# Text order instead of the scheduler's on PE, ACT and DVE, and a third buffer for the batches' rows

## The chip, the core and the metric

The kernel runs on one core of a Trainium2 chip. The metric is the device time of one execution in microseconds (us). Besides the plain times there is a profile: one execution recorded by the hardware profiler, with the start and duration of every instruction on every engine. The engines are PE (TensorE, matrix products and transposes; PEld is its loading of weights), DVE (VectorE), ACT (ScalarE), POOL (GpSimd) and SP (SyncE, which here only issues DMAs).

## What is computed

Eight batches of 2048 rows with 128 channels pass through four graph-attention layers that share one 2048 x 2048 adjacency. Each layer is preceded by a layer norm and a ReLU, and its result is added to x.

```
h = relu(layernorm(x));  x = x + layer0(h)    # GAT, then elu
h = relu(layernorm(x));  x = x + layer1(h)    # GAT
h = relu(layernorm(x));  x = x + layer2(h)    # 4 heads, scores = h_head @ h_head.T
h = relu(layernorm(x));  x = x + layer3(h)    # node weights, W, layernorm, GAT, residual, elu

GAT:    Wh = h @ W;  e[i, j] = leaky_relu(Wh[i] @ a1 + Wh[j] @ a2)
        out = softmax(where(adj > 0, e, -big)) @ Wh
heads:  e = leaky_relu(h_head @ h_head.T);  out = softmax(where(adj == 0, -inf, e)) @ h_head
```

All of it is in float32. In the second kind of layer there are four heads of 32 channels.

## The kernel before, in words

**Units and streams.** One batch in one layer is a *unit*; there are 32. Layers 0, 1 and 3 are units of class `Gat` with 16 steps, layer 2 is a unit of class `Heads` with 64 steps (four groups of 512 query rows by 16 blocks of keys). The even batches form stream a and the odd ones stream b, and the units of the two alternate: a layer 0, a layer 1, b layer 0, a layer 2, b layer 1, a layer 3, b layer 2, then layer 0 of a's next batch, b layer 3, a layer 1, b layer 0, a layer 2 and so on. So a `Heads` unit follows either a layer 0 or a layer 3 of the other stream, four times each, and a layer 3 is prepared during a layer 1 (four times) or a layer 0 (three times). The last layer 3 has nothing beside it.

**Steps.** A step has a `front` and a `back`. In `Gat`, the front makes two blocks of unnormalised attention weights on DVE (L459, twice: maximum with a spread row, times the edge mask), and the back multiplies them on PE into PSUM (L472: 16 products in the text, 32 instructions in the trace, as a float32 product takes two). In `Heads` the front makes scores on PE (L543), exponentials on ACT (L546) and the masked weights on DVE (L548); the back multiplies them with the values on PE (L557). Three `z` buffers hold the weights between front and back. In the text a front is written two steps ahead of its back (`AHEAD = 2`).

**Pieces.** While a unit runs, the next one is prepared: `begin` returns a list of pieces, and the loop calls them in proportion to the steps done (`room` is four steps fewer than the unit has). The pieces are: `first` (load x), `stats` four times (L195 and L196 per block of 128 rows), `end` (`moments_end`: L201 on DVE, the power on POOL L203, L205 on DVE), `rows` (L247, ACT), for layer 3 `scaled` (L254, DVE), for layer 2 `kept` (L258), `turned` (transposes L267 on PE, copy L270 on ACT, for layer 2 the low part L272 on DVE), for layer 2 `stacked` (16 DMAs on SP's queue, L281 and L282, that build `hi_lo` and `lo_hi`), else `project` (L291 on PE, then L396 to L398 on ACT and L303 on DVE, or for layer 3 L298 and L299), for layer 3 a second set of statistics and `normed` (L325) and `weighted` (L330), at last `spread` (L342 on PE, L343 on ACT).

**Ends of a unit.** When half of a `Gat` unit is summed, `out_first` takes the reciprocals (L409) and scales the sums out of PSUM (L413 on DVE, or L416, L417, L419 on ACT). The rest waits in a list for some steps (`later`): `out_elu` (L445, L446) for layer 0, `out_norm` (L426 to L428 on DVE, L430, L431 on ACT) and then `out_elu` and the store (L436, SP's queue) for layer 3. At the end of a group `Heads` copies its sums to `o_t` (L562, ACT), and `out` transposes them (L569), normalises (L572, L574) and adds them to x (L576).

**What sets the order.** In the kernel before, the scheduler of the tile framework orders the instructions of each engine: the text's order is a priority for it, and it may draw an instruction ahead of others. Each engine then runs its list in that order and waits at semaphores.

**Buffers.** `big` has two buffers a name unless told otherwise; x has two, `o` two, `z` three. PSUM is one tile of eight banks: scores use pairs 6, 4 and 2 in turn, sums banks 5, 6, 7 and 2, 1, 0, pieces beside a `Gat` unit banks 3 and 4 alone.

The loop that makes the text's order:

```
for s in range(u.steps):
    if s + AHEAD < u.steps:
        u.front(s + AHEAD)
    elif overlaps and not (u.layer != 2 and nxt.layer == 2):
        nxt.front(s + AHEAD - u.steps)
    elif overlaps and s == u.steps - 1:
        turn[0] = 2
        nxt.front(0)
    u.back(s, later)
    while done < total and done < total * (s + 1) / room:
        pieces[done]()
        done += 1
    pass_time(u.us)
```

Of the kernel before, what the change touches and what calls it, by code (L numbers as in the profile page):

```python
# [8 lines left out]
F32 = mybir.dt.float32  # L9
# [5 lines left out]
OP = mybir.AluOpType  # L15
PSUM = bass.MemoryType.PSUM

P = 128
HEADS = 4
HD = 32  # L20
# [15 lines left out]
def adj_preln_d4(ctx: ExitStack, tc: tile.TileContext, x, adj, w0, a0, w1, a1, w3, a3,  # L36
# [12 lines left out]
    nc = tc.nc  # L49
    B, N, C = x.shape  # L50
    NB = N // P
    HB = NB // 2
# [4 lines left out]
    const = ctx.enter_context(tc.tile_pool(name="const", bufs=1))  # L57
# [15 lines left out]
    def load(src, shape, name):  # L73
        t = const.tile(shape, F32, name=name)
        nc.scalar.dma_start(out=t, in_=src)
        return t
# [12 lines left out]
    beta_sb = load(beta.partition_broadcast(P), [P, C], "beta_sb")  # L89
# [24 lines left out]
    nc.vector.tensor_copy(tot3, pw[:, :4])  # L114
    nw1_sb = const.tile([P, NB], F32, name="nw1_sb")
    nc.vector.tensor_scalar(nw1_sb, nw_sb, 1.0, None, op0=OP.add)
    beta2_sb = const.tile([P, C], F32, name="beta2_sb")
    nc.vector.tensor_scalar(beta2_sb, beta_sb, 2.0, None, op0=OP.mult)

# [17 lines left out]
    def run(ctx, general):  # L139
        stat = ctx.enter_context(tc.tile_pool(name="stat", bufs=2))  # L140
        big = ctx.enter_context(tc.tile_pool(name="big", bufs=2))
# [10 lines left out]
        def score_banks():  # L152
            turn[0] = (turn[0] + 1) % 3
            return SCORES[turn[0]]
# [4 lines left out]
        def half_tile(name):  # L159
            return big.tile([P, HB, C], F32, tag=name, name=name)  # L160


        X = {}

        def load_x(b):
            X[b] = big.tile([P, NB, C], F32, tag="x", name="x")
            nc.sync.dma_start(out=X[b], in_=x[b].rearrange("(n p) c -> p n c", p=P))

        load_x(0)


# [36 lines left out]
        class Unit:  # L208
# [5 lines left out]
            def begin(self, banks):  # L214
# [4 lines left out]
                def first():  # L219
                    if b not in X:  # L220
                        load_x(b)
                    self.xb = X[b]
                    self.st = stat.tile([P, NB, 6], F32, tag="st", name="stx")
                    self.mv = stat.tile([P, NB, 2], F32, tag="mv", name="mvx")
# [200 lines left out]
            def out_norm(self, half, xs, a, later):  # L425
                nc.vector.tensor_add(a, a, self.wh[:, half * HB:(half + 1) * HB, :])  # L426
                nc.vector.tensor_mul(a, a, gamma_sb[:, None, :].to_broadcast([P, HB, C]))
                nc.vector.tensor_add(a, a, beta2_sb[:, None, :].to_broadcast([P, HB, C]))  # L428
                e = half_tile("oe")
                nc.scalar.activation(e, a, AF.Exp)  # L430
                nc.scalar.activation(a, a, AF.Relu)  # L431

                def last():
                    self.out_elu(xs, a, e)
                    lo = half * HB * P
                    nc.sync.dma_start(  # L436
                        out=out[self.b, lo:lo + HB * P, :].rearrange("(n p) c -> p n c", p=P),
                        in_=xs)
                    if half == 1:
                        del X[self.b]  # L440
                later(6.0, last)
# [87 lines left out]
        class Heads(Unit):  # L529
# [35 lines left out]
            def out(self, g, pair, o_t):  # L565
                lo = score_banks()
                pv = ps[:, lo, :].rearrange("p (k e) -> p k e", k=4)
                for k in range(4):
                    nc.tensor.transpose(pv[:, k, :], o_t[:, k * P:(k + 1) * P], ident)  # L569
                pv = pv.rearrange("p k (h e) -> p k h e", h=2)  # L570
                r = stat.tile([P, 4, 2, 1], F32, tag="r2", name="r2")
                nc.vector.reciprocal(r, pv[:, :, :, HD:HE])  # L572
                o = big.tile([P, 4, 2, HD], F32, tag="o", name="o")
                nc.vector.tensor_mul(o, pv[:, :, :, :HD], r.to_broadcast([P, 4, 2, HD]))  # L574
                xs = X[self.b][:, g * 4:g * 4 + 4, pair * 64:(pair + 1) * 64]
                nc.vector.tensor_add(xs, xs, o.rearrange("p k h d -> p k (h d)"))  # L576
# [10 lines left out]
        def later(us, f):  # L587
            waiting.append([us, f])
# [50 lines left out]
    ok = nc.values_load(near_i[0:1, 0:1], min_val=0, max_val=1)  # L639
    with tc.If(ok > 0) as arm:  # L640
        with ExitStack() as inner:
            run(inner, False)
    with arm.Else():
        with ExitStack() as inner:
# [25 lines left out]
```

## Time and profile before

| what | value |
|---|---|
| median of 2 runs | 3565.78 us (3564.5 to 3567.05) |
| the profiled execution | 3565.65 us, its span 3563.8 us |
| mean granted clock of PE | 0.959 |
| DMA over the span | 70.96 MB, 20 GB/s |
| largest group: L472 on PE | 1415.6 us busy, 12288 instructions |
| L557 and L543 on PE | 1014.6 and 503.6 + 440.9 us busy |
| L548 and L459 on DVE | 1171.7 and 949.0 us busy |
| L546 on ACT | 1086.3 us busy |

The span runs from the first to the last recorded instruction; the device time is 1.85 us longer. Busy time counts what an engine executes, not what it waits. In a row of the groups, "out<-in" are the program's names of the tiles, then come the count, the busy time with the mean duration of one, and the idle time of the engine just before them with what ended it. In a timeline each row has its start, its duration, the engine, line and operation, and in brackets the idle time before it and what released it. Operations of one engine can overlap in the record: the next one starts before the last has left the pipeline.

### The profile page before, as it was taken

Reading aid. Unit: us, or ns where it says so; the run is one execution under the profiler, and the core shown is the slowest. Engines: PE = TensorE matmul, PEld = TensorE weight load, DVE = VectorE, ACT = ScalarE, POOL = GpSimd, SP = SyncE. Lnnn points to the kernel's source line nnn. Section 1 sums busy time; section 2 is a strip of 40 time slices with the busy share of each in tenths; the row PEclk is TensorE's granted clock in tenths of the full one; section 3 lists DMA queues with packets and bytes.
Section 4 is the critical chain, followed back from the end, with each engine's and each line's share of the span. In section 5 each row is a group of like instructions: output and inputs, shape, how many; then the busy total and the mean of one; then the engine's idle time right before and its main releaser. Section 6 shows DMA issues by size and latency. Waiting matters only on the chain.

```text
span 3563.8 us, 53234 instructions
## 1 busy us (share of the span) xinstructions
PE 3312.8 (93%) x22669; PEld 2222.9 (62%) x22669; DVE 2673.9 (75%) x3586; ACT 1681.7 (47%) x2521; POOL 135.1 (4%) x47
## 2 busy tenths in 40 slices
PE   4798999999999899989999899999999989999997
PEld 3787337734899435943599834783379953495337
DVE  3666778777888677877787677877788767787776
ACT  4113663376422565356542276427652246624661
POOL 0000000000000000000000000000000000010000
PEclk7888999999999899999999999999999989999998
DMA  6002000300000200030000200020000020002000
GB/s 216 1 1 48 1 1 1 72 1 1 1 25 1 48 1 1 1 72 1 1 1 25 48 1 1 1 68 5 1 1 7 19 48 1 1 1 60 1 1 14
DMA packets 35511, 70.96 MB, mean 20 GB/s; under 512 B 8000, under 2 KB 25024, under 8 KB 29120
## 3 DMA queue, kind: packets, MB, share of 16 engines
q1 hardware_dynamic: 29312, 67.12, 7.3%
q8 instruction: 179, 2.93, 0.3%
q10 hardware_dynamic: 5952, 0.35, 0.1%
q14 instruction: 68, 0.56, 0.1%
HBM read 25.51 MB, written 8.39 MB: 10 GB/s over the span
## 4 chain that ended last, share of the span: by engine, by line
PE 77%; DVE 11%; ACT 5%; POOL 2%; DMA 2%; issue 2%; POOLq 0%; ACTq 0%; DVEq 0%; SPq 0%
PE ps L472 30%; PE ps L557 25%; PE ps L543 16%; DVE z L459 5%; PE ps L291 3%; POOL rstdx L203 2%; ACT z L546 2%; PE ps L267 2%; PE ps L342 1%; DVE z L548 1%; ACT hw L247 1%; DVE stx L195 1%; ACT wh L325 1%; DMA raw<-in_adj_dram 1%; PE ps L569 1%
## 5 line engine op out<-in xcount | busy, mean ns | idle before, releaser
L548 DVE TENSOR_TENSOR z<-z,edge_t 128x2048 f32<-128x2048 f32 x512 | 1171.7, 2292 | 433.6 <-ACT z L546 433.6
L472 PE MATMUL ps<-y,z 128*128 128x129 f32 x12288 | 1415.6, 276 | 4.3 <-DVE z L459 4.3
L472 PEld LDWEIGHTS ps<-y,z 128*128 128x128 f32 x12288 | 1399.9, 193 | 8.4 <-DVE z L459 4.5
L546 ACT ACTIVATE z<-ps,shift 128x1024 f32<-128x1024 f32 x1024 | 1086.3, 1111 | 428.9 <-PE ps L543 408.4
L557 PE MATMUL ps<-z,hv 128*33 128x512 f32 x4096 | 1014.6, 605 | 5.1 <-DVE z L548 4.4
L459 DVE SCALAR_TENSOR_TENSOR z<-r,cr,edge_t 128x1024 f32<-128x1024 f32 x768 | 949.0, 1275 | 92.2 <-PE ps L472 80.6
L543 PE MATMUL ps<-hi_lo 64*128 64x512 f32 x2048 | 503.6, 457 | 105.1 <-ACT z L546 99.5
L543 PEld LDWEIGHTS ps<-hi_lo 64*128 64x128 f32 x2048 | 210.4, 188 | 546.7 <-ACT z L546 425.9
L557 PEld LDWEIGHTS ps<-z,hv 128*33 128x33 f32 x4096 | 200.6, 111 | 535.7 <-issue 503.8
L247 ACT ACTIVATE hw<-x,nmrx,rstdx 128x128 f32<-128x128 f32 x512 | 203.0, 482 | 530.8 <-DVE nmrx L205 530.8
L543 PE MATMUL ps<-lo_hi,hi_lo 64*128 64x512 f32 x2048 | 440.9, 402 | 0.0
L543 PEld LDWEIGHTS ps<-lo_hi,hi_lo 64*128 64x128 f32 x2048 | 215.5, 191 | 24.6
L203 POOL TENSOR_TENSOR rstdx<-varx,neg_half 128x16 f32<-128x16 f32 x32 | 104.2, 3258 | 3123.2 <-DVE varx L201 3123.2
L416 ACT ACTIVATE oe<-ps,rs 128x128 f32<-128x128 f32 x128 | 52.7, 412 | 180.9 <-DVE rs L409 180.7
L195 DVE BATCH_NORM_STATS2 stx<-x 128x6 f32<-128x128 f32 x512 | 127.8, 267 | 12.7 <-DMA x<-in_x_dram 11.7
L267 PE MATMUL ps<-ident,hw 128*128 128x128 f32 x512 | 89.1, 299 | 45.6 <-ACT hw L247 26.8
L291 PE MATMUL ps<-rhs,h_t 128*128 128x130 f32 x768 | 117.8, 300 | 10.2 <-DVE y L303 6.7
L291 PEld LDWEIGHTS ps<-rhs,h_t 128*128 128x128 f32 x768 | 101.1, 204 | 39.9 <-ACT z L546 17.6
L419 ACT ACTIVATE oa<-ps,rs 128x128 f32<-128x128 f32 x128 | 35.3, 380 | 179.6 <-DVE rs L409 179.6
L267 PEld LDWEIGHTS ps<-ident,hw 128*128 128x128 f32 x512 | 64.1, 149 | 68.2 <-ACT hw L247 30.4
L409 DVE RECIPROCAL rs<-ps 128x3 f32<-128x3 f32 x144 | 21.5, 169 | 85.6 <-PE ps L472 85.5
L325 ACT ACTIVATE wh<-wh,nmrh,rstdh 128x128 f32<-128x128 f32 x128 | 50.9, 479 | 71.6 <-DVE sraw L319 59.0
(88 smaller groups left out, 1128.6 us busy)
## 6 DMA issues: line engine op xcount, KB each, us to landing
raw<-in_adj_dram SPq DMA_DIRECT2D x16, 1024.0 KB, 7.6
hi_lo<-h_hi SPq DMA_DIRECT2D x32, 256.0 KB, 5.1
hi_lo<-h_lo SPq DMA_DIRECT2D x32, 256.0 KB, 5.1
lo_hi<-h_lo SPq DMA_DIRECT2D x32, 256.0 KB, 5.1
lo_hi<-h_hi SPq DMA_DIRECT2D x32, 256.0 KB, 5.2
out_dram<-x SPq DMA_DIRECT2D x16, 512.0 KB, 3.3
w_sb<-in_L_gnn_W_dram ACTq DMA_DIRECT2D x3, 64.0 KB, 2.0
x<-in_x_dram SPq DMA_DIRECT2D x8, 0.5 KB, 6.3
```

The source lines that it names most:

```text
L195: nc.vector.bn_stats(out=st[:, n, :], in_=block(n))
L203: nc.gpsimd.tensor_tensor(out=rstd, in0=var, in1=neg_half, op=OP.pow)
L247: nc.scalar.activation(h, self.xb[:, n, :], AF.Relu, scale=self.rstd[:, n:n + 1], bias=self.nmr[:, n:n + 1])
L267: nc.tensor.transpose(pk[:, k, :], self.hw[half][:, k, :], ident)
L291: nc.tensor.matmul(pv[:, k, :C + 2], lhsT=self.h_t[:, n * P:(n + 1) * P], rhs=rhs, start=True, stop=True)
L325: nc.scalar.activation(self.wh[:, n, :], self.wh[:, n, :], AF.Identity, scale=self.rstd3[:, n:n + 1], bias=self.nmr3[:, n:n + 1])
L459: nc.vector.scalar_tensor_tensor(z[:, j, :], self.r[:, sl], self.cr[:, 0, jb:jb + 1], edge_t[:, jb, sl], op0=OP.max, op1=OP.mult)
L472: nc.tensor.matmul(ps[:, SUMS[half][i // 3], k * CE:(k + 1) * CE], lhsT=z[:, j, i * P:(i + 1) * P], rhs=self.y[:, jb, :], start=(jb == 0 a ...
L543: nc.tensor.matmul(ps[:, lo + h, :], lhsT=hi_lo[rows, pair, js], rhs=rhs[rows, pair, ts], start=rhs is hi_lo, stop=rhs is lo_hi)
L546: nc.scalar.activation(z[:, pair * 2:pair * 2 + 2, :], ps[:, lo:lo + 2, :], AF.Exp, bias=shift)
L548: nc.vector.tensor_mul(z, z, edge_t[:, jb, None, ts].to_broadcast([P, HEADS, 512]))
L557: nc.tensor.matmul(ps[h * 64:h * 64 + HE, pair, :], lhsT=hv[:, jb, pair * 2 + h, :], rhs=z[:, pair * 2 + h, :], start=(jb == 0), stop=(jb ...
```

## The change

PE, ACT and DVE are put under `manual_schedule` in the branch that runs: their instructions stay in the order in which the text issues them. SP and POOL are left to the scheduler. The rows x get a third buffer. `beta` is doubled in its own tile instead of a second one, and `o` has one buffer instead of two.

```diff
     nc.vector.tensor_scalar(nw1_sb, nw_sb, 1.0, None, op0=OP.add)
-    beta2_sb = const.tile([P, C], F32, name="beta2_sb")
-    nc.vector.tensor_scalar(beta2_sb, beta_sb, 2.0, None, op0=OP.mult)
+    nc.vector.tensor_scalar(beta_sb, beta_sb, 2.0, None, op0=OP.mult)
...
         def load_x(b):
-            X[b] = big.tile([P, NB, C], F32, tag="x", name="x")
+            X[b] = big.tile([P, NB, C], F32, tag="x", name="x", bufs=3)
...
             def out_norm(self, half, xs, a, later):
...
-                nc.vector.tensor_add(a, a, beta2_sb[:, None, :].to_broadcast([P, HB, C]))
+                nc.vector.tensor_add(a, a, beta_sb[:, None, :].to_broadcast([P, HB, C]))
...
-                o = big.tile([P, 4, 2, HD], F32, tag="o", name="o")
+                o = big.tile([P, 4, 2, HD], F32, tag="o", name="o", bufs=1)
...
         with ExitStack() as inner:
+            inner.enter_context(tc.manual_schedule(engines={
+                mybir.EngineType.PE, mybir.EngineType.Activation, mybir.EngineType.DVE}))
             run(inner, False)
```

## The prediction

> **What bounds the kernel now.** Line numbers are those of the profile of before. I read the page first: busy time and the chain that ended last.
>
> ```profile
> PE 3312.8 (93%) x22669; PEld 2222.9 (62%) x22669; DVE 2673.9 (75%) x3586; ACT 1681.7 (47%) x2521; POOL 135.1 (4%) x47
> PE 77%; DVE 11%; ACT 5%; POOL 2%; DMA 2%; issue 2%; POOLq 0%; ACTq 0%; DVEq 0%; SPq 0%
> ```
>
> PE is the bound and DVE the runner-up. No instruction is removed, so a new order can win only by closing pauses of PE, and lose only by opening others. I therefore asked for busy times by stage, cut at the first L472 or L557 of each unit (stage, length; then PE, PEld, DVE, ACT, POOL busy; clock; DMA).
>
> ```profile
> 264.50:324.80 60.30, 60.30 (x532) 59.41 (x530) 46.35 (x81) 13.26 (x38) 2.90 (x1) 1.00 0.25 53
> 324.80:348.20 23.40, 7.47 (x29) 4.34 (x30) 7.71 (x23) 15.19 (x36) 2.90 (x1) 0.63 0.22 46
> 554.40:626.30 71.90, 68.08 (x586) 66.92 (x585) 61.88 (x145) 19.59 (x44) 7.65 (x2) 0.98 0.01 1
> 686.60:701.70 15.10, 7.79 (x27) 4.30 (x26) 8.63 (x8) 8.84 (x13) 0.00 (x0) 0.69 0.67 157
> 912.80:980.50 67.70, 66.58 (x584) 65.44 (x585) 61.01 (x135) 23.86 (x60) 7.64 (x2) 1.00 0.00 1
> ```
>
> In an ordinary unit PE is full (60.30 of 60.30). On the way into Heads it loses most of 23.4 us (after a layer 0) or 15.1 us (after a layer 3), four times each. Where a layer 3 is prepared (554.4 and 912.8) DVE is busy 62 of 72 and 61 of 68 us: there **DVE is close to being the bound**. The timeline names the loss into Heads:
>
> ```profile
> 333.22 2.90 POOL L203 TENSOR_TENSOR rstdx<-varx,neg_half 128x16 f32<-128x16 f32 x1 [51.92 <-DVE varx L201]
> 336.43 2.41 ACT L247 ACTIVATE hw<-x,nmrx,rstdx 128x128 f32<-128x128 f32 x6 [8.21 <-DVE nmrx L205]
> 338.75 2.09 ACT L546 ACTIVATE z<-ps,shift 128x1024 f32<-128x1024 f32 x2
> 339.89 0.79 PE L543 MATMUL ps<-hi_lo 64*128 64x512 f32 x1 [12.95 <-ACT z L546]
> ```
>
> The scheduler put rows of the next unit (L247, which wait for POOL) ahead of Heads' first exponentials (L546), and PE waits 12.95 us for a bank.
>
> **What the Trainium skill says.** "TensorE: Matmul & The Clock Gate", What's actually happening: after an idle window of about 3.4 us the array runs at half rate until it has been busy as long again. The trace agrees, and shows it after 2.69 us already: eight transposes take 1.97 us for 1.05.
>
> ```profile
> 605.94 1.05 PE L342 MATMUL ps<-ident,cr 128*128 128x128 f32 x8
> 611.02 1.97 PE L342 MATMUL ps<-ident,cr 128*128 128x128 f32 x8 [2.69 <-ACT r L343]
> ```
>
> So I price a pause of over 2.6 us at itself plus 1.7 us (16 matmuls 0.214 instead of 0.111 us apart). Same page, Architectural detail: ACT and DVE take their instructions strictly in order; the 12.95 us above agree. "VectorE: DVE Perf Modes", The DRAIN you can't avoid: a read after a write on DVE itself needs a wait. The scheduler hides it by running L195 a block ahead of L196:
>
> ```profile
> 167.17 0.26 DVE L195 BATCH_NORM_STATS2 stx<-x 128x6 f32<-128x128 f32 x1
> 167.35 0.16 DVE L196 BATCH_NORM_AGGREGATE mvx<-stx 128x2 f32<-128x6 f32 x1
> 167.43 0.26 DVE L195 BATCH_NORM_STATS2 stx<-x 128x6 f32<-128x128 f32 x1
> ```
>
> A pair takes 0.26 us. The text puts every L196 right behind its own L195: 0.267 (L195) + 0.04 (what dependent L427 adds behind L426: 1.26 us apart for 1.22 long) + 0.08 (L196 to the next) = 0.39. Over 640 pairs that is 83 us more on DVE, for the same work.
>
> **The change, part by part.** In the two builds' lists PE, ACT and DVE now stand exactly in the text's order; SP and POOL keep the scheduler's. Prices: front of a Gat step, two L459 at 1.196 us, 2.39; its back, 32 L472 at 0.112, 3.57; a Heads step 2.97; statistics of four blocks 1.55; moments_end 3.5, of which DVE stands 2.97 waiting for POOL, as today:
>
> ```profile
> DVE nmrx L205 <- POOL rstdx L203: 95.0, 32, 3.5
> ```
>
> *Gat preparing a layer 3, seven times.* All 39 pieces fall in 12 of its 16 steps. Front(k) needs the z buffer that back(k-3) gives free. Let D be the end of front(k) on DVE and P that of back(k) on PE, from the start of back(0). D2 = 6.4 (Heads' last two outputs go first on DVE). Three statistics stand before front(3): D3 = 6.4 + 4.65 + 2.39 = 13.4. One and moments_end before front(4): D4 = 13.4 + 1.55 + 3.5 + 2.39 = 20.9. Four L254 before front(5): D5 = 24.3. But P2 is 10.7: backs 3 and 4 wait for DVE, and every later one with them. Then the two transposes and four projections: all use banks 3 and 4, each waits about 1.0 us for the copy of the one before, and two or three stand in one step with no back between. P7 is 44.5; PE's own work would give 33.8. After it the reciprocals with L413 (2.7), three statistics and a front: D10 = 54.4; one statistic, moments_end and 0.7 of s: D11 = 62.5. P15 is 83, with half rate after two or more pauses 85. Today 71.9 (layer 1, four times) and 67.7 (layer 0, three): 4 x 13 + 3 x 17 = **+103**.
>
> *The other Gats.* By the same steps: statistics, the previous unit's residuals and POOL's wait all stand in the first five steps. The kind of 980.5 loses 7 us (three times), that of 1045.4 3.6 (three), the first layer 1 3.5. The third x buffer is counted in: today SP's load of x waits for the store of the batch two before (PE idles 4.3, 4.1 and 4.9 us near 1077, 1930, 2780); afterwards the load stands a unit earlier. **+35.**
>
> *Into Heads.* The 12.95 us go: the next unit's rows stand at step 21. What is late next are the 16 stacking copies of SP's queue (L281, L282), one each 1.27 us, 20.5 us from the second to the last packet (310.0 to 330.5). The text puts front(0) of Heads ahead of back(15), so PE stands about 10 us for the last copy, with the 32 L472 of back(15) behind it, and out_first on DVE and ACT behind those. After a layer 0: back(10) ends 44.2 after back(0) began, the copies' second 49.7, last packet 70.2, first back of Heads 80.9 + 1.7, against 83.7 today: -1, four times. After a layer 3 SP has the store between the copies, and out_norm (3 x 1.22 on DVE) keeps ACT's L430 and L431 waiting with Heads' exponentials behind them; the third back ends at 96.3 + 1.7, against 83.1 today plus 5.4 that its step 7 loses: +9.5, four times. **+34.**
>
> *Group ends in Heads.* The step takes 6.1 us today; with the transposes of o_t ahead of the scores I find 0.6 less (17 times). At the first of seven units moments_end falls between the last multiply and the outputs' reads of PSUM, and PE waits 4.3 us for a bank; with half rate 4.5 more than today. 7 x 4.5 - 17 x 0.6 = **+21**.
>
> *Ends.* Statistics now follow all 16 adjacency blocks: +7.4. Second unit +3.7; last unit +11, as no statistics run before Heads' last output; seven changes from Heads to Gat, 0.8 each. **+28.**
>
> *The rest.* beta doubled in place: same instruction, at the start, 0.2 us at most either way. One o buffer: writer and reader are both on DVE, in order; it costs nothing as long as DVE's order covers it, else one L576 (0.4 us) an output, 26.
>
> Sum +221 on the profiled execution's 3565.65 us (span 3563.8 and 1.85 around it; median of the runs 3565.78): 3787, say **3785**. Unknown is whether the pauses add up. If half are hidden by the next, 3675; if half rate follows some 65 pauses instead of the 25 priced here, 40 x 1.7 = 68 more, 3855.
>
> **Rivals.** (1) Faster: the fronts' lead of two steps hides the lumps, and only ACT's misplaced rows go. 23.4 less three fronts' scores (4.4) is 19, and 10.7 + 5.4 is 16; four of each, 140, less 8 x 10 for the copies, plus 24 x 1.2 at group ends: 3477. It decides where front(3) ends within 10.7 us of the first back. For it speaks PE full at 264.5, against it DVE's 62 of 72 us. (2) Nearly level: the lumps cost a third and Heads wins 30: 3615. (3) The order does not take effect: 3565; the lists speak against it. (4) Much slower: DVE stays behind in the plain Gats too, 3785 + 18 x 8 = 3930.
>
> **How the numbers follow.** Forecast 0.71, (1) 0.09, (2) and (3) 0.12, (4) 0.08. The range, 3610 to 3900, takes in the forecast's bounds, half of (2) and some of (4). Two per cent, 71 us, is about what can be told from no change: faster 0.09, within 0.11, slower 0.80.
>
> **What would show it.** Right: stages like those of 554.4 and 912.8 at 83 to 86 us, PE there waiting for L459; an L196 behind each L195 at 0.3 us; on the way into Heads no L247 on ACT, and PE idle some 10 us for hi_lo or lo_hi. Wrong: those stages at 72 us or less, or PE not waiting for the copies.

## The result, and the profile after

The changed kernel takes 3789.27 us (median of 2 runs, 3787.88 to 3790.66), 1.0627 of the kernel before (95% interval 1.0581 to 1.0672). Its span in the profile is 3786.1 us, 222.3 more, at a mean granted clock of 0.944 (before 0.959). One line was taken away at the top of the kernel, so line numbers are one lower than before: L459 is now L458, L472 is L471, L543 is L542.

The page of the changed kernel, busy time and the chain that ended last:

```profile
PE 3325.6 (88%) x22669; PEld 2246.7 (59%) x22669; DVE 2743.8 (72%) x3586; ACT 1681.6 (44%) x2521; POOL 117.0 (3%) x47
PE 62%; DVE 18%; ACT 5%; issue 2%; POOL 2%; SPq 2%; DMA 1%; POOLq 0%; DVEq 0%; ACTq 0%
```

The same number of instructions, and DVE 70 us busier; PE stands idle 460.5 us instead of 251.0, and its share of the chain falls from 77 to 62%, DVE's grows from 11 to 18%. What PE waits for is in the view of waits (engine, line, releaser: us in total, times, longest). The kernel before, then the changed one:

```profile
PE ps L543 <- ACT z L546: 99.5, 34, 12.9
...
PE ps L472 <- DVE z L459: 4.3, 1, 4.3
```

```profile
PE ps L471 <- DVE z L458: 114.9, 58, 6.2
PE ps L542 <- DMA hi_lo<-h_lo: 50.5, 17, 4.2
PE ps L542 <- DVE o L573: 38.8, 24, 4.3
PE ps L542 <- ACT z L545: 35.2, 12, 6.2
...
PE ps L542 <- DMA lo_hi<-h_hi: 25.5, 16, 3.2
```

The exponentials behind misplaced rows (12.9 us at a time) are gone. In their place PE waits for fronts on DVE, for the stacking copies and, at group ends, for DVE's reads of PSUM. Of the 35.2 us of L545 that are left 27 have another cause, shown below. By stage (length; PE, PEld, DVE, ACT, POOL busy; clock; DMA), these are the stages of the changed kernel that answer to the five shown in the prediction:

```profile
276.90:337.20 60.30, 57.49 (x502) 56.02 (x501) 47.46 (x79) 12.49 (x35) 2.90 (x1) 1.00 0.20 43
337.20:358.20 21.00, 10.56 (x52) 8.05 (x52) 2.82 (x4) 8.08 (x20) 0.00 (x0) 0.67 0.39 81
569.10:654.00 84.90, 70.47 (x578) 68.84 (x577) 65.94 (x152) 19.24 (x43) 5.80 (x2) 0.94 0.00 1
714.30:735.20 20.90, 10.97 (x55) 8.16 (x57) 2.83 (x4) 6.17 (x12) 0.00 (x0) 0.67 0.47 101
954.70:1039.90 85.20, 70.17 (x578) 68.73 (x577) 65.58 (x144) 24.20 (x62) 5.80 (x2) 0.92 0.00 1
```

Where a layer 3 is prepared the stage takes 84.9 and 85.2 us instead of 71.9 and 67.7. The reason is seen on DVE in the first of them, which begins at 569.1 (timeline: start, us, engine, line; in brackets the idle time before it and what ended it):

```profile
575.15 0.29 DVE L194 BATCH_NORM_STATS2 stx<-x 128x6 f32<-128x128 f32 x1
575.48 0.18 DVE L195 BATCH_NORM_AGGREGATE mvx<-stx 128x2 f32<-128x6 f32 x1
575.58 0.26 DVE L194 BATCH_NORM_STATS2 stx<-x 128x6 f32<-128x128 f32 x1
...
579.91 2.45 DVE L458 SCALAR_TENSOR_TENSOR z<-r,cr,edge_t 128x1024 f32<-128x1024 f32 x2
...
583.99 0.18 DVE L200 TENSOR_SCALAR varx<-mvx 128x16 f32<-128x16 f32 x1
587.27 0.17 DVE L204 SCALAR_TENSOR_TENSOR nmrx<-mvx,rstdx 128x16 f32<-128x16 f32 x1 [3.10 <-POOL rstdx L202]
587.37 2.47 DVE L458 SCALAR_TENSOR_TENSOR z<-r,cr,edge_t 128x1024 f32<-128x1024 f32 x2
```

Twelve pairs of statistics stand between two fronts, each begun 0.40 us after the one before, then four more and 3.10 us of waiting for POOL. Front(3) ends 13.2 us after the first back, front(4) at 20.7 (587.37 + 2.47 - 569.1), while PE, with backs of 3.57 us, could have begun on them at 10.7 and 14.3.

On the way into Heads, on PE:

```profile
336.63 0.47 PE L542 MATMUL ps<-lo_hi,hi_lo 64*128 64x512 f32 x1 [1.22 <-DMA lo_hi<-h_hi]
...
339.10 0.79 PE L542 MATMUL ps<-hi_lo 64*128 64x512 f32 x1 [2.00 <-DMA hi_lo<-h_lo]
...
344.13 0.76 PE L542 MATMUL ps<-hi_lo 64*128 64x512 f32 x1 [4.25 <-DMA hi_lo<-h_lo]
...
346.55 0.76 PE L542 MATMUL ps<-lo_hi,hi_lo 64*128 64x512 f32 x1 [1.53 <-DMA lo_hi<-h_hi]
347.24 5.91 PE L471 MATMUL ps<-y,z 128*128 128x129 f32 x32
```

The scores of Heads' first step follow the copies one by one, 9.5 us in the mean of eight (76.0 over 8), and the last back of the Gat unit (L471, 347.24) stands behind them. It then takes 5.91 us for its 32 instructions, where early, below, shows 3.84: the first 19 come 0.21 us apart, the others 0.11.

After a layer 3 more follows, some 5 us after the first back of Heads (735.16):

```profile
739.89 1.22 DVE L425 TENSOR_TENSOR oa<-oa,wh 128x1024 f32<-128x1024 f32 x1
...
743.72 1.06 ACT L429 ACTIVATE oe<-oa 128x1024 f32<-128x1024 f32 x1 [6.26 <-DVE oa L427]
...
745.77 4.11 ACT L545 ACTIVATE z<-ps,shift 128x1024 f32<-128x1024 f32 x4
746.92 0.79 PE L542 MATMUL ps<-hi_lo 64*128 64x512 f32 x2 [6.22 <-ACT z L545]
```

ACT stands 6.26 us at L429 for out_norm's three operations on DVE, Heads' exponentials stand behind it, and PE waits 6.22 us for a bank; this comes four times.

### The profile page after: what moved, and what is told of

It reads as the page before. It is cut to its first block, busy times and chain, and to the rows that moved or that the text cites. A ratio compares the mean times of both kernels' runs of the same rounds, so it can differ in the third digit from the quotient of the medians.

```text
span 3786.1 us, 53159 instructions
## 1 busy us (share of the span) xinstructions
PE 3325.6 (88%) x22669; PEld 2246.7 (59%) x22669; DVE 2743.8 (72%) x3586; ACT 1681.6 (44%) x2521; POOL 117.0 (3%) x47
## 4 chain that ended last, share of the span: by engine, by line
PE 62%; DVE 18%; ACT 5%; issue 2%; POOL 2%; SPq 2%; DMA 1%; POOLq 0%; DVEq 0%; ACTq 0%
PE ps L556 22%; PE ps L471 22%; PE ps L542 14%; DVE z L458 8%; ACT z L545 2%; PE ps L290 2%; DVE z L547 2%; POOL rstdx L202 2%; DMA lo_hi<-h_hi 1%; DVE stx L194 1%; DVE mvx L195 1%; PE ps L341 1%; PE ps L266 1%; SPq L280 1%; SPq L281 1%
## 5 line engine op out<-in xcount | busy, mean ns | idle before, releaser
L471 PE MATMUL ps<-y,z 128*128 128x129 f32 x12288 | 1465.4, 282 | 115.3 <-DVE z L458 114.9
L471 PEld LDWEIGHTS ps<-y,z 128*128 128x128 f32 x12288 | 1445.0, 199 | 131.5 <-DVE z L458 128.0
L545 ACT ACTIVATE z<-ps,shift 128x1024 f32<-128x1024 f32 x1024 | 1087.7, 1114 | 610.5 <-PE ps L542 605.7
L458 DVE SCALAR_TENSOR_TENSOR z<-r,cr,edge_t 128x1024 f32<-128x1024 f32 x768 | 942.4, 1277 | 85.4 <-PE ps L471 60.6
L556 PE MATMUL ps<-z,hv 128*33 128x512 f32 x4096 | 995.0, 608 | 8.2 <-DVE z L547 8.2
L542 PE MATMUL ps<-hi_lo 64*128 64x512 f32 x2048 | 473.6, 452 | 127.4 <-DMA hi_lo<-h_lo 50.5
L542 PEld LDWEIGHTS ps<-hi_lo 64*128 64x128 f32 x2048 | 196.3, 186 | 534.2 <-ACT z L545 335.1
L246 ACT ACTIVATE hw<-x,nmrx,rstdx 128x128 f32<-128x128 f32 x512 | 206.0, 488 | 559.9 <-DVE nmrx L204 559.9
L542 PE MATMUL ps<-lo_hi,hi_lo 64*128 64x512 f32 x2048 | 419.9, 397 | 25.5 <-DMA lo_hi<-h_hi 25.5
L542 PEld LDWEIGHTS ps<-lo_hi,hi_lo 64*128 64x128 f32 x2048 | 199.4, 188 | 53.6 <-issue 24.8
L202 POOL TENSOR_TENSOR rstdx<-varx,neg_half 128x16 f32<-128x16 f32 x32 | 92.9, 2902 | 3281.6 <-DVE varx L200 3281.6
L266 PE MATMUL ps<-ident,hw 128*128 128x128 f32 x512 | 77.6, 292 | 41.4 <-ACT hw L246 24.5
L195 DVE BATCH_NORM_AGGREGATE mvx<-stx 128x2 f32<-128x6 f32 x512 | 93.2, 182 | 17.8
L302 DVE TENSOR_TENSOR y<-ps,y 128x512 f32<-128x512 f32 x64 | 44.1, 688 | 84.1 <-ACT cr L397 83.9
```

Source lines behind the costliest of these rows:

```text
L195: nc.vector.bn_aggr(out=mv[:, n, :], in_=st[:, n, :])
L202: nc.gpsimd.tensor_tensor(out=rstd, in0=var, in1=neg_half, op=OP.pow)
L246: nc.scalar.activation(h, self.xb[:, n, :], AF.Relu, scale=self.rstd[:, n:n + 1], bias=self.nmr[:, n:n + 1])
L266: nc.tensor.transpose(pk[:, k, :], self.hw[half][:, k, :], ident)
L458: nc.vector.scalar_tensor_tensor(z[:, j, :], self.r[:, sl], self.cr[:, 0, jb:jb + 1], edge_t[:, jb, sl], op0=OP.max, op1=OP.mult)
L471: nc.tensor.matmul(ps[:, SUMS[half][i // 3], k * CE:(k + 1) * CE], lhsT=z[:, j, i * P:(i + 1) * P], rhs=self.y[:, jb, :], start=(jb == 0 a ...
```

## Experiments

In the table the stages are measured from the first L472 or L557 of a unit to that of the next, and averaged over n; *into Heads* is the Gat unit before a Heads. All in us; the last line is the span. The first two units and the last are not in the table. Line numbers move with each edit, so the views name the same operation by other lines. The medians of the kernel before, taken again beside each group of runs, were 3563.6 to 3567.5 us, so nothing is read into 4 us of the whole time between one kernel and another; *start* alone, which waits for the adjacency, differs by as much where its text is the same (107.5 to 111.5).

| stage | n | before | x3 | dve | peact | after | stats | early | split | slots | tuned2 |
|---|---|---|---|---|---|---|---|---|---|---|---|
| start | 1 | 102.0 | 103.1 | 109.5 | 106.8 | 107.5 | 106.6 | 111.5 | 110.3 | 109.8 | 105.1 |
| layer 1 preparing a layer 3 | 4 | 71.2 | 70.4 | 81.9 | 75.7 | 84.5 | 81.0 | 84.6 | 83.5 | 77.7 | 68.9 |
| layer 0 preparing a layer 3 | 3 | 67.3 | 67.3 | 82.2 | 74.5 | 85.3 | 81.8 | 85.3 | 84.8 | 79.0 | 71.7 |
| layer 0 into Heads | 4 | 83.6 | 83.6 | 77.4 | 77.8 | 81.6 | 79.6 | 72.2 | 77.2 | 81.2 | 70.2 |
| Heads after layer 0 | 4 | 206.7 | 206.3 | 212.7 | 208.1 | 210.1 | 210.4 | 210.8 | 206.9 | 210.6 | 205.6 |
| layer 3 into Heads | 4 | 75.4 | 76.5 | 78.0 | 79.3 | 81.2 | 79.0 | 68.2 | 79.2 | 81.2 | 66.7 |
| Heads after layer 3 | 3 | 211.7 | 206.9 | 217.6 | 211.2 | 219.5 | 219.4 | 219.0 | 213.1 | 219.1 | 208.9 |
| other layer 3 | 3 | 64.9 | 70.8 | 66.9 | 72.1 | 72.9 | 71.8 | 72.9 | 70.7 | 72.9 | 68.3 |
| other layer 1 | 3 | 71.4 | 64.6 | 70.4 | 67.0 | 74.2 | 70.7 | 74.2 | 72.0 | 72.6 | 68.3 |
| last Heads and what follows it | 1 | 231.3 | 231.9 | 246.0 | 238.1 | 249.5 | 244.3 | 249.2 | 249.6 | 248.6 | 236.2 |
| span | | 3563.8 | 3546.8 | 3707.8 | 3621.9 | 3786.1 | 3721.3 | 3702.0 | 3714.6 | 3734.3 | 3481.0 |

**x3: the buffer without the order.**

```diff
-            inner.enter_context(tc.manual_schedule(engines={
-                mybir.EngineType.PE, mybir.EngineType.Activation, mybir.EngineType.DVE}))
```

> The changed kernel with the scheduler left in charge of all engines: only the third buffer of x, the one buffer of o and beta doubled in place remain. Theory: the load of x no longer waits for the store of the batch two before, so the three idle stretches of PE near 1077, 1930 and 2780 us (4.3, 4.1, 4.9) go and nothing else changes: 3552 us, 0.4% faster. Rival: PE's idle time comes back a little later (the scheduler orders everything anew, o has one buffer): 3565 within 5 us, or slower by up to 26 if the single o buffer holds back an output of a group.

Measured: 3547.37 us (5 runs), ratio 0.9956 (0.9942 to 0.9969). The size is about as expected (3552) and the single buffer of o costs nothing that shows, but "nothing else changes" was wrong. The three pauses are gone and those units fall from 71.4 to 64.6; the units ahead of them rise from 64.9 to 70.8, since statistics and rows of the new batch are now made there. Most of the net gain is in Heads after a layer 3 (211.7 to 206.9, three times): in the trace the first such unit makes 12 statistics and no rows, where it made 28 and 16 before. The unit ahead of it, which makes 32 rows instead of 16 now, takes 1 us more.

**dve and peact: the order on DVE alone, and on PE and ACT alone.**

```diff
-            inner.enter_context(tc.manual_schedule(engines={
-                mybir.EngineType.PE, mybir.EngineType.Activation, mybir.EngineType.DVE}))
+            inner.enter_context(tc.manual_schedule(engines={mybir.EngineType.DVE}))
```

In peact the set is PE and Activation.

> The changed kernel with the text's order on DVE alone; the scheduler orders PE and ACT. Theory of the prediction: what costs in Gat units is DVE's order (statistics and POOL's wait ahead of the fronts), 103 us where a layer 3 is prepared and some 30 in the other Gats, so 3690 to 3710 us here, those stages at 80 us or more. Rival: it is the order of PE and ACT that costs (banks waited for within a step, the copies ahead of the back): then 3565 to 3600 here, and the loss shows in the kernel with PE and ACT in the text's order.

> The changed kernel with the text's order on PE and ACT; the scheduler orders DVE. Theory: Gat units stay near their times of before (stages of 68 to 74 us where a layer 3 is prepared), since DVE may put fronts ahead of statistics; what remains is PE standing for the stacking copies ahead of the last back, and ACT's exponentials behind out_norm: some 20 to 40 us, less 13 for the third x buffer: 3570 to 3600 us. Rival: PE's and ACT's order is what costs: 3700 us or more.

Measured: dve 3706.94 us, 1.0398 (1.0382 to 1.0414); peact 3623.6 us, 1.0167 (1.0151 to 1.0182). Against x3 that is 159.6 and 76.2 us; together 235.8, and both orders at once cost 3789.27 - 3547.37 = 241.9. **In the total the two losses add up.** By stage they do not, as is shown below. The waits of dve, then of peact:

```profile
PE ps L471 <- DVE z L458: 94.1, 57, 3.6
...
PE ps L542 <- ACT z L545: 14.9, 26, 1.0
PE ps L542 <- DMA hi_lo<-h_lo: 14.0, 9, 1.9
```

```profile
PE ps L542 <- DMA hi_lo<-h_lo: 55.5, 19, 4.6
PE ps L542 <- ACT z L545: 26.3, 12, 4.0
...
PE ps L471 <- DVE z L458: 9.3, 7, 4.7
```

PE waits for fronts at length only where DVE keeps the text's order (94.1 us, against 9.3), and for the copies at length only where PE and ACT do (55.5 us for hi_lo, against 14.0). The stages that prepare a layer 3 lose 91 of dve's 161 us (4 x 11.5 and 3 x 14.9 over x3), and 43 of peact's 75 (4 x 5.3 and 3 x 7.2). So peact missed its 3570 to 3600 us: the theory expected these stages to stay. Either order alone does away with the 12.9 us of misplaced exponentials. Together 91 and 43 are 134 us, but both orders at once cost these stages only 110 (4 x 14.1 and 3 x 18.0): there the losses overlap. Ahead of Heads it is the other way. After a layer 0 each order alone gains 6 us a unit over x3, and both together gain 2. The agreement of the totals is in part such cancelling. PE's order and ACT's were not taken apart for this text.

**stats: bn_stats a block ahead of bn_aggr within a piece.**

```diff
+            nc.vector.bn_stats(out=st[:, n0, :], in_=block(n0))
             for n in range(n0, n1):
-                nc.vector.bn_stats(out=st[:, n, :], in_=block(n))
+                if n + 1 < n1:
+                    nc.vector.bn_stats(out=st[:, n + 1, :], in_=block(n + 1))
                 nc.vector.bn_aggr(out=mv[:, n, :], in_=st[:, n, :])
```

> The changed kernel with bn_stats written one block ahead of bn_aggr within each piece of four blocks. Theory: a pair takes 0.26 us again instead of 0.395 for three of four blocks, so a piece of four takes 1.15 instead of 1.58 us; a Gat preparing a layer 3 has eight such pieces and gains 3 to 4 us (seven times), the other Gats four pieces and 1 to 2 us (eight times), the start 1.7, Heads nothing: 35 to 45 us less than the changed kernel, 3745 to 3755 us. Rival: DVE only waits longer for POOL or PE elsewhere in the unit, and the time stays at 3785 to 3790 us.

Measured: 3725.96 us, 1.0457 (1.0441 to 1.0473), 63 us less than the changed kernel. DVE in stats:

```profile
573.86 0.26 DVE L196 BATCH_NORM_STATS2 stx<-x 128x6 f32<-128x128 f32 x1
574.03 0.16 DVE L197 BATCH_NORM_AGGREGATE mvx<-stx 128x2 f32<-128x6 f32 x1
574.12 0.26 DVE L196 BATCH_NORM_STATS2 stx<-x 128x6 f32<-128x128 f32 x1
```

A pair is 0.26 us again (573.86 to 574.12), and DVE is busy 2691.0 us instead of 2743.8. The stages that prepare a layer 3 gain 3.5 each, as expected. More came than the 35 to 45 us, mainly from 3.5 in each other layer 1 and 5.2 in the last Heads and what follows it; the eight units into Heads gain 2.0 and 2.1 each.

**early: layer 2 prepared in 9 steps instead of 12.**

```diff
-            room = u.steps - 4
+            room = 9 if overlaps and u.layer != 2 and nxt.layer == 2 else u.steps - 4
```

> The changed kernel with the preparation of layer 2 packed into 9 of the 16 steps instead of 12, so that the stacking copies start some three steps (11 us) earlier. Theory of the prediction: on the way into Heads PE stands for the last copy (76 us in all in the profile, 9.5 each time) because front(0) of Heads is ahead of back(15); with the copies earlier this wait goes, less some 2 us each for statistics that stand closer together: the step that took 18.4 to 19.6 us takes 8 to 10, and the whole 45 to 65 us less than the changed kernel, 3725 to 3745 us. Rival: PE stands there for DVE or ACT as well (fronts made late by the statistics), and the copies are only the last of several: 3775 us or more.

Measured: 3703.48 us, 1.0387 (1.0369 to 1.0404), 86 us less than the changed kernel. The way into Heads in early:

```profile
342.64 1.00 PE L542 MATMUL ps<-lo_hi,hi_lo 64*128 64x512 f32 x2
343.57 3.84 PE L471 MATMUL ps<-y,z 128*128 128x129 f32 x32
348.95 0.50 PE L542 MATMUL ps<-hi_lo 64*128 64x512 f32 x2 [1.54 <-ACT oa L416]
```

No wait for a copy is left ahead of the last back, which runs at full rate (3.84 us for 32). The units into Heads gain 9.4 us after a layer 0 and 13.0 after a layer 3, 90 in all, more than the 45 to 65 expected; *start* takes 4 us back. In sum this is the eight pauses of 9.5 us with the prediction's 1.7 for the half rate behind each (8 x 11.2 = 90), but not one by one: the waits for copies that went are 9.0 to 9.3 and 9.7 to 10.3 us, and why the units after a layer 3 gain 3 us beyond theirs was not pursued. The copies were the cause, not the last of several.

**split: the power on POOL and the product that needs it in two pieces, two pieces apart.**

```diff
                 add(end)
-                add(lambda: None)
+                for _ in range(2):
+                    add(lambda: None)
+                add(end2)
```

`norm_end`, the second one of a layer 3, is divided in the same way.

> The changed kernel with moments_end in two pieces, the power on POOL in one, the product that needs it two pieces later, so that DVE has other work between. Theory: DVE stands 124 us for POOL in the changed kernel; where a layer 3 is prepared twice 3 us a unit (seven times, 42), in the other Gats and at the start 3 each of which half counts, and at the group end in Heads where PE waited 4 us for a bank that DVE was late to read (seven times, 28 to 31): 60 to 80 us less than the changed kernel, 3710 to 3730 us. Rival: only the group ends count, since in Gats the pieces that follow need the product at once and are late by as much: 3755 to 3760 us.

Measured: 3717.48 us, 1.0426 (1.0409 to 1.0444), 72 us less than the changed kernel. The size was right and its place was not. The stages that prepare a layer 3 gain 1.0 and 0.4 us, 5 of the 42 expected; Heads gains 3.2 and 6.4 (32 in all, mainly at the group ends, where PE's waits for the outputs on DVE fall from 38.8 to 14.9 us), the units into Heads 4.4 and 2.0 (26). DVE's waits for POOL in split:

```profile
DVE nmrh L207 <- POOL rstdh L202: 24.1, 8, 3.0
DVE nmrx L207 <- POOL rstdx L202: 20.3, 10, 3.1
```

Where a layer 3 is prepared, three or four pieces run in a step. For the second set of statistics "two pieces later" is the same step: DVE meets the product at once, and all eight waits for rstdh are as before (24.1 us). For the first set a front does stand between: of rstdx's waits 20.3 of 99.6 us are left, and front(4) ends at 17.4 us instead of 20.7. But the rows come a step later now, PE's transposes wait 2.32 us for L259, and back(6) begins at 35.3 us as before (35.4). Taking a wait away on DVE gained nothing where PE's own pieces were next in line.

**slots: the pieces of a layer 3 set to steps by hand.** (The list has 38 such lines.)

```diff
+                    at(0, stats, 0)
+                    at(0, stats, 1)
+                    at(1, stats, 2)
+                    at(1, stats, 3)
+                    at(1, end)
+                    k = 2
+                    at(k, end2)
+                    at(k, rows, 0)
...
+                    at(13, spread, 1)
```

> The changed kernel with one part rewritten: the pieces that prepare a layer 3 are set to steps by hand (two pieces of statistics a step instead of three, the product after POOL's power a step later, one or two of PE's pieces a step, all done by step 13). Statistics are still made pair by pair, and the other preparations are as in the changed kernel. Theory of the prediction: the 103 us of these seven stages come from lumps of three or four pieces in one step, not from DVE's sum; the stages fall from 84.5 and 85.3 us to 72 to 76 and the time by 60 to 85 us, to 3700 to 3725 us. Rival: DVE's load itself is too much for the stage (some 64 us with pairs at 0.395), and any order leaves them at 80 us or more: 3750 us or more.

Measured: 3737.96 us, 1.0480 (1.0464 to 1.0496), 51 us less than the changed kernel: between the theory and the rival. The stages gain 6.8 and 6.3 us and stop at 77.7 and 79.0. The lumps that this list still has are seen in its timeline:

```profile
585.98 2.47 DVE L515 SCALAR_TENSOR_TENSOR z<-r,cr,edge_t 128x1024 f32<-128x1024 f32 x2
586.24 3.78 POOL L202 TENSOR_TENSOR rstdx<-varx,neg_half 128x16 f32<-128x16 f32 x1 [172.67 <-DVE varx L200]
...
590.05 0.17 DVE L207 SCALAR_TENSOR_TENSOR nmrx<-mvx,rstdx 128x16 f32<-128x16 f32 x1 [1.60 <-POOL rstdx L202]
...
596.35 1.24 PE L272 MATMUL ps<-ident,hw 128*128 128x128 f32 x4 [2.32 <-DVE hw L259]
```

A front stands between power and product now, but POOL takes 3.78 us beside it instead of 2.90, and DVE still waits 1.60. And PE's transposes stand ahead of a back while their rows are still scaled on DVE. That DVE's load binds was the rival. DVE is busy 65.3 us of 78.0 and of 79.6 in two of these stages, so it is not full; whether any order brings this same load to 72 us no run shows, as tuned2 below also makes the load smaller.

**tuned, tuned2: all of these in one text.** Besides, three quarters of layer 3's first statistics are made in Heads at its group ends:

```diff
                 nc.vector.tensor_add(xs, xs, o.rearrange("p k h d -> p k (h d)"))
+                if pair == 1 and g < 3:
+                    later(2.6, lambda: self.group_stats(g, 0))
+                    later(8.0, lambda: self.group_stats(g, 2))
```

> The text's order on PE, ACT and DVE, with the text rewritten: bn_stats a block ahead, moments_end in two pieces, layer 2 prepared in 9 steps, the pieces of layer 3 set to steps by hand (no step with more than two of PE's pieces), three quarters of layer 3's first statistics made in Heads at the ends of its groups, the operations of out_norm and out_elu one a step, the first statistics among the adjacency's blocks. Theory: the order loses only by lumps on DVE and by copies and POOL's wait ahead of PE's work, so the gains add up (65 for the statistics as measured, 70, 55, and 30 to 60 for the rest): 3520 to 3580 us. Rival: a fixed order cannot follow the real durations, and the gains overlap: 3620 us or more.

In tuned the second operation of out_elu stands a step behind statistics of layer 1 that read its rows, so these are taken from rows without it, and the result is not that of the layers: tuned's time is no measure of this computation. It took 3477.77 us, 0.9751 (0.9734 to 0.9767). In tuned2 the operation stands ahead of them.

> The rewritten text of the run before, but the two operations of out_elu stay together, since statistics of the next layer read these rows a step later. Expected: 3470 to 3490 us, ratio 0.975 to the kernel before, since a pair of 1.2 us more or less in one step is nothing that a lead of two steps does not take.

Measured: tuned2 3483.2 us (5 runs), 0.9766 (0.9753 to 0.9779), **faster than both kernels**, and below the 3520 to 3580 us that were expected of the rewriting. Two stages of tuned2 that prepare a layer 3:

```profile
549.30:618.70 69.40, 67.08 (x579) 66.15 (x578) 59.62 (x128) 19.12 (x43) 7.64 (x2) 0.98 0.01 1
894.80:966.50 71.70, 67.11 (x579) 66.03 (x578) 59.28 (x120) 23.75 (x61) 7.64 (x2) 0.98 0.01 1
```

PE is busy 67.1 of 69.4 us beside 59.6 us of DVE, 6 us less DVE work than in the changed kernel (65.9), since pairs are short and some statistics stand in Heads. All three engines are in the text's order, as in the changed kernel. With the original text fixing them costs 242 us (x3 to the changed kernel); with this one it gains 42 (tunedsched, next, to tuned2). It was the text's order that lost, not the fixing of it.

**tunedsched, tunedact, tunedpeact: tuned2's text with fewer engines fixed.** The edit is the set of engines as above: none, ACT, PE and ACT.

> The same rewritten text with the scheduler in charge of all engines. Theory: the scheduler still draws instructions ahead of others (rows of the next unit ahead of Heads' exponentials), so the way into Heads stays at 75 to 84 us, but the statistics made in Heads relieve the stages that prepare a layer 3: 3500 to 3545 us. Rival: with the text in a good order the scheduler follows it, 3470 to 3490 us as with the text's order; or its order gains nothing from the text: 3547 us.

> The rewritten text with the text's order on ACT alone; the scheduler orders PE and DVE. Theory: what the scheduler does badly is one thing, rows of the next unit on ACT ahead of Heads' exponentials, and what it does well is PE and DVE in the Gat units. So the way into Heads falls from 82.2 and 73.3 us to the text's 70.2 and 66.7 (74 us in eight), and the Gat units stay as with the scheduler: 3450 to 3470 us. Rival: PE and DVE, ordered for another ACT, lose as much elsewhere, or the misplaced work only moves to PE or DVE: 3500 to 3530 us.

> The rewritten text with the text's order on PE and ACT; the scheduler orders DVE. Theory: the same gain on the way into Heads, while the Gat units that prepare no layer 3 lose some 2 us each to the fixed order of PE (as they did with the text of the changed kernel, 72.1 and 67.0 against 70.8 and 64.6): 3465 to 3490 us, level with the text's order on all three. Rival: PE's order matters for the way into Heads as much as ACT's, and this one is the fastest, under 3455 us.

Measured: tunedsched 3525.13 us, 0.9882 (0.9867 to 0.9897); tunedact 3486.82 us, 0.9779 (0.9766 to 0.9792); tunedpeact 3527.5 us, 0.9893 (0.9878 to 0.9908). The waits of tunedsched, then of tunedact (L610 are Heads' scores, L613 its exponentials):

```profile
PE ps L610 <- ACT z L613: 77.3, 24, 11.3
```

```profile
PE ps L610 <- ACT z L613: 19.6, 26, 1.0
```

With ACT fixed the misplaced exponentials go (11.3 to 1.0 us), and the ways into Heads fall from 82.2 and 73.3 us to 67.3 and 68.6: 78 us, what the theory gave. But Heads itself grows from 206.0 to 211.3 and from 205.7 to 209.8, 33 us, so with small losses elsewhere 38 are left. The expected 3450 to 3470 missed that return. The trace shows where it is: the first step of Heads takes 5.7 to 7.6 us, where at most 4.4 in tunedsched, and a later one after a layer 0 takes 5.1. In the first such unit out_elu's two operations stand on DVE ahead of a step's masked weights there. No run tests this. With PE fixed too (expected 3465 to 3490), all is level with the scheduler: into Heads 70.7 and 72.5, but 71.4 and 72.9 where a layer 3 is prepared (68.8 and 68.9 with the scheduler). So the theory fell, and with it its rival, that PE's order matters as much.

## Why the prediction was right

3785 us was forecast and 3789 measured. By its steps, each from its stages:

- **Gat preparing a layer 3**, +103: measured +53.1 and +53.9, 107. The recursion held at each point, in all seven: front(3) at 13.2 us (13.4 predicted), front(4) at 20.7 (20.9), front(5) at 24.1 (24.3), the end of back(7) at 44.7 to 45.9 (44.5), front(10) at 53.0 to 55.2 (54.4), front(11) at 62.5 to 64.0 (62.5), the end of back(15) at 84.2 to 85.7 (85 with half rate). dve shows that DVE's order alone makes 91 us here, stats that the pairs are 3.5 us of each stage, slots that lumps are six to seven more.
- **A pair of statistics** at 0.39 us: 0.395 in the trace. "VectorE: DVE Perf Modes", The DRAIN you can't avoid, was cited for the reason, that a reader behind its writer on DVE needs a wait; stats, where another instruction stands between, agrees: 0.26 us a pair, and 63 us of the time.
- **The other Gats**, +35: measured +36.3, by kind 8.0 for 7, 2.8 for 3.6 and 3.7 for 3.5. How much the third buffer took off is not shown. Its 16 us in x3 lie mostly in Heads after a layer 3, where the text's order keeps 16 statistics and 16 rows.
- **Into Heads**, +34: measured about +31. After a layer 0 the first back comes 2.0 us sooner (1 forecast). After a layer 3 the third back ends at 97.4 to 97.6 us (98.0 forecast) for 83.4 before, but the 5.8 us that before loses a few steps later are saved three times, not four. The copies came out as priced, 9.5 us each for "about 10", and early takes them away. The wait of L429 for out_norm came where it was placed.
- **Handovers** and **last preparation** under *ends*, 0.8 each and +11: measured 0.8 and 12.1.
- **Group ends**, +21: measured about +19. The step at the first one, with what the next step takes beyond 2.97 us, is 10.2 to 11.1 us, 10.6 in the mean, for 10.6 forecast (6.1 + 4.5); the later ones gain 0.7 each for 0.6. split, which takes POOL's wait away there, brings the first down to 5.4. The cause stands in the changed kernel's timeline:

```profile
408.77 2.90 POOL L202 TENSOR_TENSOR rstdx<-varx,neg_half 128x16 f32<-128x16 f32 x1 [110.92 <-DVE varx L200]
411.70 0.18 DVE L204 SCALAR_TENSOR_TENSOR nmrx<-mvx,rstdx 128x16 f32<-128x16 f32 x1 [3.10 <-POOL rstdx L202]
411.80 0.20 DVE L571 RECIPROCAL r<-ps 128x8 f32<-128x8 f32 x1
412.03 0.42 DVE L573 TENSOR_TENSOR o<-ps,r 128x256 f32<-128x256 f32 x1
412.51 0.50 PE L542 MATMUL ps<-hi_lo 64*128 64x512 f32 x2 [3.98 <-DVE o L573]
```

- **Start and second unit**, +11.1 (7.4 and 3.7): measured 5.5 and 3.3, 8.8.
- **That the pauses add up** was named as the unknown. They do in the sense of the forecast, each counted on top of the others in its own stage: 222 us for 221. That dve and peact add up in the total does not show it, since by stage they do not.
- Rival (1) fell at the point that it named: front(3) ends at 13.2 us, not within 10.7, and the lead of two steps does not hide the lumps. The misplaced rows did go, as it said. Rival (4), which counts 18 other Gats where there are 17, did not come: they lost what was forecast and no more, and the last unit's backs take 60.0 us as before.

Part of the closeness is luck: the misses of the single terms, from -3 to +4 us, nearly cancel. Two thoughts in it were too simple, without harm to the sum. The stage was called close to being DVE-bound for its 62 us of DVE in 72; in tuned2, with 59.6 us of DVE, it is PE that fills it (67.1 of 69.4). And PE and ACT's own share, a third of the loss, was seen in the copies and in banks 3 and 4 but not told apart from DVE's.

## What to carry to other kernels

In this kernel fixing the engines' order cost what the text's lumps were worth. Add up, step by step, what stands ahead of each producer, and compare it with its lead. Fix one engine at a time when measuring, and look at which engine holds each instruction that the scheduler misplaces. Here a text with even steps, held on three engines, and the same text held on ACT alone both gave 0.977 to 0.978 of the time before, where the original text held on three gave 1.063.

## Not expected of the hardware

The power on POOL (128x16, L202) takes 2.90 us while DVE stands waiting for it: in the changed kernel all 32 for rstdx lie between 2.899 and 2.917. In split and in tuned2 the median of the 32 is 3.78. The lines of slots above show one of these, 0.26 us behind the start of a front. In split there are also others, beside Heads' masked weights:

```profile
403.80 2.90 POOL L202 TENSOR_TENSOR rstdx<-varx,neg_half 128x16 f32<-128x16 f32 x1 [100.72 <-DVE varx L200]
404.22 2.29 DVE L561 TENSOR_TENSOR z<-z,edge_t 128x2048 f32<-128x2048 f32 x1 [0.59 <-ACT z L559]
```

What counts in all 560 powers of the 14 profiles is the DVE instruction that is running when POOL starts. Where that is one with two inputs in SBUF, as half a front is (183 times, with 0.96 to 1.11 us of it left), the power takes longer by what is left of it less 0.14 us. Where such an instruction starts after POOL (masked weights 21 times, 0.06 to 0.42 us behind, fronts three times), the power keeps its 2.90 us, and the masked weights their 2.29 to 2.31. A copy (hv from hw, nine times) lengthens it as a front does, by what is left of the copy less 0.14 us.

The Trainium skill ("SBUF — State Buffer", Who interferes with whom) says that a DVE instruction with two SBUF inputs contends with a GpSimd instruction that reads SBUF, and that the order of issue decides who blocks. The traces agree where POOL is second: it loses the rest of one DVE instruction. Where POOL was first, DVE lost nothing. So DVE work put between power and product buys less than its own length if it starts just ahead of POOL: in slots 2.47 us of it took 3.10 us of waiting down to 1.60.
